# Position logits read from a turned copy of the queries, all between the key products

## The chip, the core and the metric

The kernel runs on one core of a Trainium2 chip. The metric is device time in microseconds (us), the median of several runs. A profiled execution gives a trace of every instruction, from which the views below are taken.

## What is computed

The input is eight images of 32 x 32 pixels with 512 channels. Two layers follow, each a group norm, an attention over all 1024 pixels and a residual sum. The first has 16 heads of 32 channels, the second 4 heads of 128 channels. Everything is in 32-bit floats. Only the second layer matters for the change. Cut to that:

```python
q = x @ Wq * scale
k = (x @ Wk).reshape(B, L, heads, kd).transpose(0, 2, 3, 1)
v = (x @ Wv).reshape(B, L, heads, kd).transpose(0, 2, 1, 3)
scores = attn_q @ k
pos = relative_logits(pos_q, pos_emb_w, pos_emb_h)
scores = scores + pos.reshape(B, heads, L, L)
attn = jax.nn.softmax(scores, axis=-1)
out = attn @ v
```

`relative_logits` adds, for a query at row x and column y of the image, one logit for each key column (from `pos_emb_w`, shifted by y) and one for each key row (from `pos_emb_h`, shifted by x). So all queries of one image column share a 32-wide window of `pos_emb_w`, and all queries of one image row share a window of `pos_emb_h`.

## The kernel before

Activations lie channels on partitions, pixels along the free dimension: a block is 128 partitions x 4 chunks x 1024 pixels. Blocks come from one pool with eight buffers (`block`, line 75). PSUM has a pool of three banks that most products share (`bank`, line 81), a tile `ps` of four banks with one buffer for the logits of the first layer (line 692), and one bank `acc`.

The 512 x 512 products with the weights are cut into halves and done with seven half-size products instead of eight (`seven`, line 407). A unit is one half of the output channels; its seven products go to three PSUM banks x, y and z in the order x, y, x, y, z, y, z. Each product is 16 TensorE passes (or 32 of half the length for the values), spread over four strips of 32 columns of the array (`by_columns`, line 327); a float matmul takes two passes. ScalarE, VectorE and GpSimd take the results out (lines 416 to 444 and the class `Plain`, lines 560 to 583): line 573 is ScalarE's copy of x, line 576 VectorE's sum from y, line 579 VectorE's sum from z, line 583 GpSimd's sum of two intermediate tiles, one of which is line 435's copy of z. All four quarters of a unit's output are there only when all four have run.

The first layer's attention (`attention_0`, line 685) runs in 64 steps a batch, and each step computes the logits of four heads into `ps` (line 698), takes their exponential on ScalarE (line 713), multiplies the exponentials of the step before with the values (line 724) and sums them on VectorE (line 736). Since `ps` has one buffer, line 698 of a step waits until line 713 of the step before has read it.

Between these steps `side_by_side` (line 1138) weaves the other work in by cost: each part yields how much it costs, and pieces are taken until their share of the total is reached. The other work of an iteration is, for the batch before, the rest of the first layer, the second layer's products (`second`, line 1058) and then the first batch's steps of the second attention (`attention_1`, line 811); the last batch runs its second layer with nothing beside it. `woven` (line 1126) lays a side sequence between the pieces of a main one: from piece `start` on, in each period of `gap` pieces, one piece of the side at each place in `places`.

`second` makes the queries, then the keys and the values with the position logits woven between. The position logits (`position_logits`, line 768) come in four groups a batch. A group takes one of the three shared banks, fills it with 16 matmuls (8 of line 782 for the image's columns, 8 of line 789 for its rows, 32 passes together, two strips for each line), casts four pieces of it to the block `posT` on ScalarE (line 802) and puts the four rests beside them on VectorE (line 807). The bank is free when the last of these has read it. With a start of 2 and a gap of 7, two groups stand between the keys' 14 products, two between the values'. Later line 822 adds the position logits to the second layer's logits.

Instructions are recorded in this order, and a scheduler then lays each engine's own sequence out and sets the waits; each engine runs its sequence in that order.

Of the kernel before, what the change touches and what calls it, by code (L numbers as in the profile page):

```python
# [27 lines left out]
def quick_path(  # L28
# [23 lines left out]
    nc = tc.nc  # L52

    B, IH, IW, C = x.shape
# [20 lines left out]
    def block(name, shape=None, dtype=F32):  # L75
        return mem.tile(shape or [P, CC, N], dtype, tag="block", name=name, bufs=BLOCKS)

    def chunks(block):
        return [block[:, i, :] for i in range(CC)]

    def bank(name, shape=None):
        return psum.tile(shape or [P, NB], F32, tag="bank", name=name, bufs=3)
# [38 lines left out]
    HC, HN = CC // 2, NB // 2  # L121
# [49 lines left out]
    ORDER = [0, 5, 1, 4, 6, 2, 3]  # L171
# [202 lines left out]
    def forms(x, name, room=None):  # L374
        got = []

        def whole():
            got.append((yield from forming(x, name, room)))

        run(whole())  # L380
        return got[0]
# [25 lines left out]
    def seven(fs, u, rows, sink, name, hook=None):  # L407

        product = taken(fs, u, rows)
        x = bank(f"x_{name}")
        product(x, 0, True)
        p1 = snapshot("e1", f"p1_{name}")
        nc.scalar.copy(p1, x)
        yield HC
        y = bank(f"y_{name}")
        product(y, 5, True)
        a = snapshot("es1", f"a_{name}")  # L420
        reader[0] = begun[0] = nc.vector.tensor_add(a, y, p1)
        sink.early(p1, a)
        yield HC
        product(x, 1, False)
        sink.c11(x)
        yield HC
        product(y, 4, False)
        b = snapshot("es1", f"b_{name}")
        reader[0] = half_done[0] = nc.vector.tensor_add(b, y, p1)
        sink.middle(b)  # L430
        yield HC
        z = bank(f"z_{name}")
        product(z, 6, True)
        p7 = snapshot("e1", f"p7_{name}")
        nc.scalar.copy(p7, z)  # L435
        yield HC
        product(y, 2, False)
        sink.c12(y, p1)
        if hook is not None:
            hook()  # L440
        yield HC
        product(z, 3, False)
        sink.c21(z, a)
        sink.c22(b, p7)
        yield HC
# [178 lines left out]
    def halves(x, u):  # L624

        return [[x[n * HC + u][:, h * NB : (h + 1) * NB] for h in range(NH)] for n in range(2)]

    def project_T(fs, m, y, name, units=(0, 1)):

        for u in units:  # L630
            stream.unit(m, False, u)
            yield from seven(fs, u, False, Plain(halves(y, u)), f"{name}_{u}")

    def project_rows(fs, m, y, name, hook=None, units=(0, 1)):

        for u in units:
            dst = [
                [y[:, h * (NT // 2) + 2 * u :, n * HN : (n + 1) * HN][:, :2] for h in range(NH)]
                for n in range(2)
            ]  # L640
            stream.unit(m, True, u)
            yield from seven(
                fs,
                u,
                True,
                Plain(dst, lambda t: t.rearrange("p (t n) -> p t n", n=HN)),
                f"{name}_{u}",
                hook if u else None,
            )
# [115 lines left out]
        yield 1  # L765
        finish(*state.pop("ended"))

    def position_logits(q, posT, b):

        qv = q.rearrange("p h (x y) -> p h x y", y=IW)
        by_y = posT.rearrange("p h (x s r) -> p r s h x", r=2, s=IW // 2)
        by_x = posT.rearrange("p h (s r y) -> p r s h y", r=2, s=IH // 2)
        G = NB // (IW * H1)
        for t in range(IW // (2 * G)):
            pp = bank(f"pp_{b}_{t}", [P, G, H1, 32])
            for g in range(G):
                for r in range(2):  # L780
                    s = 2 * (t * G + g) + r
                    nc.tensor.matmul(
                        pp[64 * r : 64 * r + 32, g],
                        pw_sb[:, IW - 1 - s : 2 * IW - 1 - s],
                        qv[:, :, :, s],
                        start=True,
                        stop=True,
                    )
                    nc.tensor.matmul(  # L789
                        pp[64 * r + 32 : 64 * r + 64, g],  # L790
                        ph_sb[:, IH - 1 - s : 2 * IH - 1 - s],
                        qv[:, :, s, :],
                        start=True,
                        stop=True,
                    )
            parts = []
            for r in range(2):
                for u, view in enumerate((by_y, by_x)):
                    view = view[:, r, t * G : (t + 1) * G]
                    rows = slice(64 * r + 32 * u, 64 * r + 32 * u + 32)  # L800
                    rests = slice(64 * (1 - r) + 32 * u, 64 * (1 - r) + 32 * u + 32)
                    nc.scalar.copy(view[rows], pp[rows])  # L802
                    parts.append((view[rests], pp[rows], view[rows].bitcast(F32)))

            yield -2
            for i, (rest, logits, greater) in enumerate(parts):
                nc.vector.tensor_sub(rest, logits, greater)  # L807
                if i % 2:
                    yield 0
# [248 lines left out]
    def second(b, st):  # L1058

        if "xn1" in st:  # L1060
            fs, sums = st.pop("xn1"), st.pop("sums1")
        else:
            fs, sums = forms(st.pop("x1"), f"xn1_{b}"), iter(())
        q = st["ao"] = block(f"q1_{b}")
        yield from woven(project_T(fs, WQ1, chunks(q), f"q1_{b}"), sums, 0, 2 * len(ORDER), (0, 3))
        posT = block(f"posT_{b}", dtype=F32R)
        k = chunks(block(f"k1_{b}"))
        v = block(f"v1_{b}", [P, NT, C])
        keys_and_values = chain(
            project_T(fs, WK1, k, f"k1_{b}"), project_rows(fs, WV1, v, f"v1_{b}")  # L1070
        )

        yield from woven(
            keys_and_values, position_logits(q, posT, b), 2, len(ORDER), (0, 1, 2)
        )
        st["at"] = (q, k, v, posT, b)

# [48 lines left out]
    def woven(main, side, start, gap, places=(0,)):  # L1126

        for at, cost in enumerate(main):
            if at >= start and (at - start) % gap in places:
                cost += next(side, 0)  # L1130
            yield cost
        yield from side
# [21 lines left out]
    def chain(*parts):  # L1154
        for part in parts:
            yield from part
# [20 lines left out]
    WP, WQ1, WK1 = Matrix(w_proj, 0, "p"), Matrix(Wq, 0, "q1"), Matrix(Wk, 0, "k1")  # L1177
# [45 lines left out]
    for b in range(B + 1):  # L1223
        rest, total = [], 0
        s = [None] * 2 + states + [None] * 2
# [9 lines left out]
        if last is not None:  # L1235
# [17 lines left out]
            else:  # L1253
                rest.append(chain(woven(other_keys(b, here), norm, 1, 1), marked()))
                total += PRODUCT // 2
            rest.append(later(second, b - 1, last))
            total += SECOND
            shared = here is not None and coming is None
# [522 lines left out]
```

## Time and profile before

| | |
|---|---|
| runs, us | 3816.88, 3814.26, 3814.05 (median 3814.26) |
| profiled execution, span from first to last instruction, us | 3815.0 |
| granted TensorE clock, mean | 0.998 |
| busy TensorE, VectorE, ScalarE, GpSimd, us | 3786.7, 2574.9, 1761.8, 660.0 |
| line 782, position logits of the columns | 512 passes, 69.7 us of union |
| line 789, position logits of the rows | 512 passes, 42.5 us of union |
| line 802, casts on ScalarE | 128, 106.1 us |
| line 807, subtractions on VectorE | 128, 112.0 us |

The profiled execution's own time is its span. The views call TensorE's matmuls PE, its weight loads PEld, VectorE DVE, ScalarE ACT, GpSimd POOL and SyncE SP. A row of a group has the line, engine and operation, output and inputs, shapes and count, then busy time in us and the mean in ns, then the engine's idle time just before and who ended it. A row of the timeline has the start in us from the span's start, the time it took, the instruction, and in brackets the idle time before it. Passes of TensorE overlap, and their ends are modelled, so its cost is read from the steps between starts.

### The profile page before, as it was taken

What the parts mean: (1) busy time and instruction counts of PE and PEld (TensorE: products, weight loads), DVE (VectorE), ACT (ScalarE), POOL (GpSimd) and SP (SyncE); (2) the same over time, 40 slices, a digit from 0 to 9 for tenths busy, and PEclk for the clock granted to TensorE, in tenths of its full rate; (3) what the DMA queues carried; (4) which work ended last, traced back from release to release, by engine and by line L of the source; (5) the groups of instructions that cost most, each with busy time, mean ns of one, the idle gap of its engine ahead of it and who ended that gap; (6) DMA issues with size and microseconds to landing.
All of it is one profiled execution on the core that took longest, in us unless ns stands there. A gap on an engine that the chain in (4) does not pass through costs nothing. (4 is left out here: it accounts for less than half of the span.)

```text
span 3815.0 us, 79937 instructions
## 1 busy us (share of the span) xinstructions
PE 3786.7 (99%) x34478; PEld 1376.4 (36%) x34478; DVE 2574.9 (67%) x2967; ACT 1761.8 (46%) x1830; POOL 660.0 (17%) x397
## 2 busy tenths in 40 slices
PE   9999999999999999999999999999999999999998
PEld 4232244323443234432343323433234332334353
DVE  6778665586656866569665686656866569665545
ACT  2555544445444454444544445444454445553132
POOL 1342101131101310013111131111310113001201
PEclk9999999999999999999999999999999999999999
DMA  6132120232202312034120241103411033110321
GB/s 186 62 105 70 39 56 10 71 102 53 56 12 92 86 46 56 16 93 93 38 53 19 94 95 40 45 23 98 91 41 40 26 98 77 33 37 31 110 41 26
DMA packets 482985, 234.74 MB, mean 62 GB/s; under 512 B 269600, under 2 KB 461376, under 8 KB 481600
## 3 DMA queue, kind: packets, MB, share of 16 engines
q1 hardware_dynamic: 470992, 213.74, 20.8%
q0 software_dynamic: 2608, 13.70, 1.0%
q8 instruction: 274, 4.49, 0.5%
q10 hardware_dynamic: 9024, 2.10, 0.3%
q14 instruction: 87, 0.71, 0.1%
HBM read 170.72 MB, written 58.72 MB: 60 GB/s over the span
## 5 line engine op out<-in xcount | busy, mean ns | idle before, releaser
L736 DVE TENSOR_TENSOR e_room<-e_room 128x2048 f32<-128x2048 f32 x448 | 1078.6, 2407 | 396.4 <-ACT e_room L713 393.7
L713 ACT ACTIVATE e_room<-ps 128x2048 f32<-128x2048 f32 x512 | 961.8, 1879 | 788.5 <-PE ps L698 744.2
L698 PE MATMUL ps<-q,k 32*64 32x512 f32 x8192 | 577.7, 613 | 0.2 <-ACT e_room L713 0.2
L724 PE MATMUL acc<-e_room,v 128*32 128x512 f32 x4096 | 545.8, 604 | 0.0
L824 ACT ACTIVATE e<-ps 128x512 f32<-128x512 f32 x512 | 305.7, 597 | 507.4 <-PE ps L822 436.3
L821 PE MATMUL ps<-q,k 128*128 128x512 f32 x1024 | 525.0, 594 | 0.2 <-DVE posT L807 0.2
L833 PE MATMUL acc<-e,v 128*128 128x512 f32 x1024 | 522.0, 593 | 0.3 <-ACT e L824 0.3
L679 POOL TENSOR_TENSOR q<-q,su 128x512 f32<-128x512 f32 x127 | 198.2, 1560 | 1524.8 <-DVE su L675 1423.5
L844 DVE TENSOR_TENSOR es<-es,e 128x512 f32<-128x512 f32 x384 | 290.5, 757 | 250.9 <-ACT e L824 248.3
L822 PE MATMUL ps<-posT,sel 128*128 128x512 f32 x512 | 406.6, 794 | 0.0
L821 PEld LDWEIGHTS ps<-q,k 128*128 128x128 f32 x1024 | 192.6, 190 | 230.1 <-issue 218.5
L698 PEld LDWEIGHTS ps<-q,k 32*64 32x64 f32 x8192 | 120.4, 129 | 391.3 <-issue 223.1
L833 PEld LDWEIGHTS acc<-e,v 128*128 128x128 f32 x1024 | 193.1, 189 | 147.3 <-issue 92.6
L724 PEld LDWEIGHTS acc<-e_room,v 128*32 128x32 f32 x4096 | 81.3, 108 | 411.4 <-issue 364.1
L659 DVE STREAM_TRANSPOSE tu<-su 128x512 f32<-128x512 f32 x128 | 90.6, 708 | 98.2 <-ACT su L657 96.5
L822 PEld LDWEIGHTS ps<-posT,sel 128*128 128x128 f32 x512 | 97.3, 190 | 122.5 <-issue 122.5
L657 ACT COPY su<-sums 128x512 f32<-128x512 f32 x128 | 74.9, 585 | 131.1 <-PE sums L746 81.3
L807 DVE TENSOR_TENSOR posT<-pp,posT 32x512 fp32r<-32x512 f32 x128 | 112.0, 875 | 32.2 <-ACT posT L802 30.9
L583 POOL TENSOR_TENSOR k<-b_k,p_k 128x512 f32<-128x512 f32 x32 | 50.7, 1584 | 477.7 <-ACT p_k L435 467.0
L802 ACT CAST posT<-pp 32x512 fp32r<-32x512 f32 x128 | 106.1, 829 | 46.0 <-PE pp L789 44.9
L583 POOL TENSOR_TENSOR v<-b_v,p_v 128x512 f32<-128x512 f32 x32 | 51.5, 1611 | 436.5 <-ACT p_v L435 436.5
L583 POOL TENSOR_TENSOR q<-b_q,p_q 128x512 f32<-128x512 f32 x32 | 67.9, 2121 | 255.2 <-ACT p_q L435 255.2
(223 smaller groups left out, 4542.3 us busy)
## 6 DMA issues: line engine op xcount, KB each, us to landing
w_qkv<-ws_qkv SPq DMA_DIRECT2D x168, 128.0 KB, 2.5
d<-x0T SPq DMA_DIRECT2D x32, 512.0 KB, 3.2
x1T<-d SPq DMA_DIRECT2D x32, 512.0 KB, 5.7
d<-x1T SPq DMA_DIRECT2D x32, 512.0 KB, 3.6
x2T<-d SPq DMA_DIRECT2D x32, 512.0 KB, 6.2
w_qkv<-in_L_conv_w_qkv SPq DMA_DIRECT2D x126, 128.0 KB, 2.2
out<-ot SPq DMA_DIRECT2D x240, 64.0 KB, 2.0
xs<-in_x SPq DMA_DIRECT2D x224, 64.0 KB, 2.5
```

The source lines that it names most:

```text
L583: nc.gpsimd.tensor_tensor(self.dst[1][1], s(b), s(p7), op=ALU.add)
L679: engine.tensor_tensor(dst, dst, su, op=ALU.mult)
L698: nc.tensor.matmul(ps[some, r, :], k[m][rows, j * P + 64 * i : j * P + 64 * i + 64], q[m][rows, h * NB : (h + 1) * NB], start=True, stop=True,
L713: nc.scalar.activation(e, ps, AF.Exp, scale=D0 ** -0.5)
L724: nc.tensor.matmul(acc[r * D0 : (r + 1) * D0, :], v[:, j, c0 : c0 + D0], e[:, r, :], start=(j == blocks[0]), stop=(j == blocks[-1]),)
L736: summed[0] = nc.vector.tensor_add(state["esum"], state["esum"], e)
L807: nc.vector.tensor_sub(rest, logits, greater)
L821: nc.tensor.matmul(ps, k[h][:, keys], q[:, h, queries], start=True, stop=False)
L822: nc.tensor.matmul(ps, sel_flat[:, keys], posT[:, h, queries], start=False, stop=True)
L824: nc.scalar.activation(e, ps, AF.Exp, scale=1.0 / math.sqrt(D1))
L833: nc.tensor.matmul(acc, v[:, j, h * D1 : (h + 1) * D1], e, start=(j == 0), stop=(j == NT - 1),)
L844: added[0] = nc.vector.tensor_add(state["esum"], state["esum"], e)
```

## The change

A new block `turned` gets a copy of the second layer's queries in which each image is turned over: pixels column by column instead of row by row. ScalarE makes it, one chunk of 128 x 1024 at a time, two after each of the queries' two units, four a batch. Line 782 (783 in the changed kernel) reads its queries from there: for one image column, 32 elements in a row for each of four heads, where it read 128 elements that were 32 apart. The matmuls, their number, shapes and results are the same. The gap of the weave becomes 3, so that all four groups of position logits stand between the keys' products, from the third on, one group every three products, and none between the values'.

```diff
-    def position_logits(q, posT, b):
+    def position_logits(q, turned, posT, b):
...
         qv = q.rearrange("p h (x y) -> p h x y", y=IW)
+        tv = turned.rearrange("p h (y x) -> p h y x", x=IH)
...
                         pw_sb[:, IW - 1 - s : 2 * IW - 1 - s],
-                        qv[:, :, :, s],
+                        tv[:, :, s, :],
...
         q = st["ao"] = block(f"q1_{b}")
-        yield from woven(project_T(fs, WQ1, chunks(q), f"q1_{b}"), sums, 0, 2 * len(ORDER), (0, 3))
+        turned = block(f"turned_{b}")
+
+        def queries():
+            for u in range(2):
+                yield from project_T(fs, WQ1, chunks(q), f"q1_{b}", (u,))
+                for m in (u, u + HC):
+                    nc.scalar.copy(
+                        turned[:, m, :].rearrange("p (y x) -> p y x", x=IH),
+                        q[:, m, :].rearrange("p (x y) -> p y x", y=IW),
+                    )
+
+        yield from woven(queries(), sums, 0, 2 * len(ORDER), (0, 3))
...
         yield from woven(
-            keys_and_values, position_logits(q, posT, b), 2, len(ORDER), (0, 1, 2)
+            keys_and_values, position_logits(q, turned, posT, b), 2, 3, (0, 1, 2)
         )
```

## The prediction

> **What bounds the kernel now.** I read the page's busy shares first, then the groups by line, then the timeline of one batch of the second layer.
>
> ```profile
> PE 3786.7 (99%) x34478; PEld 1376.4 (36%) x34478; DVE 2574.9 (67%) x2967; ACT 1761.8 (46%) x1830; POOL 660.0 (17%) x397
> L713 ACT ACTIVATE e_room<-ps 128x2048 f32<-128x2048 f32 x512 | 961.8, 1879 | 788.5 <-PE ps L698 744.2
> L698 PE MATMUL ps<-q,k 32*64 32x512 f32 x8192 | 577.7, 613 | 0.2 <-ACT e_room L713 0.2
> ```
>
> PE is busy for 99% and its idle time before the first layer's logits (L698) is 0.2 us. So a PE microsecond removed is one gained, and a PE wait added is one lost. ACT idles, but its exponentials (L713, 1.88 us) work on one PSUM tile `ps` (one buffer), so the next L698 waits for the exponential before. The timeline of batch 2's queries, second unit, shows the room:
>
> ```profile
> 1360.58 0.59 ACT L435 COPY p_q<-z_q 128x512 f32<-128x512 f32 x1 [0.85 <-PE z_q L331]
> 1361.25 2.70 POOL L583 TENSOR_TENSOR q<-b_q,p_q 128x512 f32<-128x512 f32 x1 [0.58 <-ACT p_q L435]
> ...
> 1362.74 0.68 DVE L576 TENSOR_TENSOR q<-y_q,p_q 128x512 f32<-128x512 f32 x1
> ...
> 1363.33 1.88 ACT L713 ACTIVATE e_room<-ps 128x2048 f32<-128x2048 f32 x1 [2.16 <-PE ps L698]
> ...
> 1365.24 2.29 DVE L736 TENSOR_TENSOR e_room<-e_room 128x2048 f32<-128x2048 f32 x1 [1.82 <-ACT e_room L713]
> 1365.87 1.11 PE L698 MATMUL ps<-q,k 32*64 32x512 f32 x16
> ...
> 1367.45 0.68 DVE L579 TENSOR_TENSOR q<-z_q,a_q 128x512 f32<-128x512 f32 x1
> ```
>
> The exponential ends at 1365.21 and the next L698 starts at 1365.87: 0.66 us to spare.
>
> The operation that the change is about:
>
> ```profile
> L782 PE MATMUL pp<-q,pw_sb x512: 393/433/452, 431.1 to 3639.6; 128*32 128x128 f32 x171
> ```
> ```profile
> L789 PE MATMUL pp<-q,ph_sb x512: 272/273/299, 431.1 to 3639.0; 128*32 128x128 f32 x171
> ```
> (ns, least/median/most.) L782 moves 128 queries 32 elements apart, L789 the same number in runs of 32: 433 against 273 ns. ACT pays for such steps too. Of the four casts of one group, the first writes 32 elements apart, the second runs:
>
> ```profile
> L802 ACT CAST posT<-pp x1: 1087/1087/1087, 1377.2 to 1377.2; 32x512 fp32r<-32x512 f32 x1
> ```
> ```profile
> L802 ACT CAST posT<-pp x1: 576/576/576, 1378.3 to 1378.3; 32x512 fp32r<-32x512 f32 x1
> ```
>
> [...]L583 took 2.70 us beside L736 above, 1.28 us at its quickest. [...]the trace's ACT copies of 512 and exponentials of 2048 elements (585, 1879 ns) give 0.842.
>
> **PE's gain.** A group of position logits is 32 passes (16 matmuls, two passes each) in four column strips side by side, eight to a strip. A strip of L782 starts its passes on average 0.249 us apart (first to last start 1.68 to 1.79 us for seven steps), so a group takes 1.99 us; where the column strips of L789 are not held back, theirs start 0.109 us apart (1374.99, 1375.10, 1375.21, 1375.32). With both in runs: 8 x 0.109 = 0.87 us. There are 8 batches x 4 groups: 32 x (1.99 - 0.87) = **35.8 us gained**. Bounds: nothing below 0.87 is shown. From above, products with 256 columns run 32 passes in 1.73 us, so PE can be fed at least this fast: a gain of at least 32 x 0.26 = 8 us. I take 35.8, since L789's strips did run at 0.109 with all four strips in flight.
>
> **The copies on ACT.** 32 are added (two a unit, two units a batch), 128 x 1024, read 32 apart and written in a row. The trace shows no such read. Lower end: in a row, 585 + 512 x 0.842 = 1.02 us[...]. Upper end: the cast's surcharge, (1087 - 576)/512 = 1.0 ns an element, 1.02 + 1.02 = 2.04. I take 2.0, because L782 shows the surcharge on reads and the cast shows it on ACT. 32 x 2.0 = 64 us of ACT time, which its idle 54% could hold; what costs is the place. In the built order of the changed kernel the first copy stands ahead of the exponential that follows the unit's sixth product, and waits for POOL L583 and DVE L576; the second waits for DVE L579. All exponentials queue behind.
>
> Walk through the unit above. POOL ends at 1363.95; the copy runs 1364.0 to 1366.0; the exponential ends at 1367.9 instead of 1365.21; the next L698 starts at 1368.0, not 1365.87: **2.1 us lost** (copy + 0.1). The sum on DVE (L736) stands ahead of L579 and needs that exponential: it ends at 1370.2, L579 at 1370.9, the second copy at 1372.9, the next exponential at 1374.8. PE meanwhile has attention (0.88) and two products (1.83 + 1.72) and would go on at 1373.5: **1.45 lost** (copy - 0.57). So 3.55 a unit: the second unit of batches 1 to 5, 17.8 us. Batch 0's first unit has one product there instead of two: 2.1 + 3.15 = 5.2; its second has two and a sum, 2.1 + 0.4 = 2.5. In the first unit of batches 1 to 5 both copies stand ahead of one exponential: in batch 2, L576 ends at 1343.34, copies to 1347.4, exponential to 1349.3, next L698 at 1349.35 instead of 1346.54: 2.8 x 5 = 14. Batch 6, with other attention steps between, 3.1 + 2; batch 7 has no exponentials: 0.4. Sum: 17.8 + 7.7 + 14 + 5.1 + 0.4 = **45 us lost**. With 1.02 us copies the same walk gives 18.
>
> **The closer groups.** They now come every three products instead of seven. A group holds one of three PSUM banks until its four casts (3.36 us) and four subtractions (3.53, begun after the last cast) are done: 7 us. The built order of batch 2, from the start of the product ahead of group one: PE does that product (to 1.7), the group (2.6), two products (6.1), L698 and attention (8.0), a product (9.8), and wants a bank for group two. ACT casts group one from 2.8 to 6.1, DVE subtracts from 6.15 to 9.7: free in time. Group two ends at 10.7; a product, attention and two products follow (17.9), while its casts end at 14.2 and its subtractions at 17.8: in time again. Behind group three's casts (19.0 to 22.3) and a copy stands an exponential that could start at 21.8 and starts at 22.9; the next L698 wants its end at 24.3 and gets it at 24.9, 0.6 us late. Group four, wanted at 28.6, finds its bank free since 25.9. So 0.7 x 7 = 5 us. In batch 7, without attention between, group two is wanted three products after group one, at 7.75, and gets the bank at 9.7; group three is wanted at 15.8 and gets it at 17.8; before group four a product waits 0.9 for a copy behind the casts, and the group 1.9 for the subtractions: 6.8 us. Before the change, a bank made PE wait some 0.4 us there four times:
>
> ```profile
> 3618.10 1.93 PE L331 MATMUL x_v<-w_v,x1T 128*32 128x256 f32 x32 [0.25 <-PE z_k L331]
> ```
>
> That is 6.8 - 1.7 = 5. Together **10 lost** (bounds 3 and 31: nothing late but batch 7 in part; or 1 us more for each of 21 groups). The value products, free of groups, no longer wait for a bank: in six batches the last ran 0.4 us long, **2.4 back**. The moved steps issue no DMA, and L802 and L807 are the same instructions as before. The tile `turned` takes one of eight blocks; the values' block needs it back, and the last group has read it before the first value product, so no wait. Weight loads on SP keep their order, and its queue is passed by nothing.
>
> **Sum** on the profiled execution: 3815.0 - 35.8 + 45 + 10 - 2.4 = 3831.8. Its span is 0.7 above the median (3814.26) with nothing that matters around it, so 3831.
>
> **Rivals.**
> - *The copies are cheap*: 1.02 us each, 18 lost instead of 45: 3804. For it: no read 32 apart by ACT is in the trace. Against: PE reads and ACT writes both pay. The sign turns at about 1.4 us a copy. This is the one that ends faster.
> - *PE is fed too slowly*: with L782's reads mended, 32 weight loads and 32 passes take 1.73 us a group, gain 8: 3859. For it: L698 takes 1.044 us for 16 passes[...]. Against: the 0.109 us steps.
> - *The banks bind*: the 0.1 us margins are lost, 1 us at 21 groups: 3852. For it: margins so thin; DVE's L736 can take 3.05 us instead of 2.29. Against: that was beside POOL, which is not due there.
>
> **Chances.** Forecast 0.56 (own range 3822 to 3843), cheap copies 0.22, slow feed 0.10, banks 0.12. The measurement tells 0.2%, 7.6 us: under 3806.6 is faster, over 3821.9 slower. Faster: most of the cheap copies and a little of the forecast, 0.17; same: their rest and the forecast's low end, 0.13; slower 0.70. The range goes from the cheap copies' 3803 to 3855 between the last two; outside it are half of those cases' chances at most.
>
> **What would show it.** L783's matmuls at 273 ns and groups near 0.9 us; the copies (line 1072) at 2.0 us; "L698 <- ACT e_room" with waits of 2 to 3 us some 26 times, in the queries' stretch alone; small waits in the keys' stretch. Wrong if the copies take 1.0 us, if L698 doesn't wait for ACT though they take 2, or if a group stays near 2 us.

## The result and the profile after

| kernel | median, us | range | executions |
|---|---|---|---|
| before | 3814.16 | 3813.34 to 3816.88 | 4 |
| changed | 3839.46 | 3835.74 to 3840.41 | 4 |

The changed kernel is slower by 25.3 us: ratio 1.0063, 95% interval 1.0049 to 1.0077. The forecast was 3831 (3803 to 3855).

The page of the changed kernel, whose lines answer to the first three that were shown of before (line numbers behind the new line 774 are one higher):

```profile
span 3833.9 us, 80001 instructions
...
PE 3760.0 (98%) x34478; PEld 1350.4 (35%) x34478; DVE 2577.0 (67%) x2967; ACT 1820.0 (47%) x1862; POOL 667.2 (17%) x397
...
L713 ACT ACTIVATE e_room<-ps 128x2048 f32<-128x2048 f32 x512 | 961.9, 1879 | 719.6 <-PE ps L698 684.7
...
L698 PE MATMUL ps<-q,k 32*64 32x512 f32 x8192 | 578.7, 613 | 33.8 <-ACT e_room L713 33.8
```

PE works 26.7 us less, yet the span is 18.9 us longer: its idle time went from 28.3 to 73.9 us. The last line says where most of that lies: ahead of L698 it was idle for 33.8 us, ended by ACT's exponential L713. Before it was 0.2.

The rows of the operation that was mended, with least, median and most in ns:

```profile
L783 PE MATMUL pp<-turned,pw_sb x512: 269/273/297, 436.7 to 3638.6; 128*32 128x128 f32 x171
```
```profile
L790 PE MATMUL pp<-q,ph_sb x512: 272/273/298, 436.7 to 3638.6; 128*32 128x128 f32 x171
```

L783 now costs what L790 costs, 273 ns. The passes of a strip start 0.109 us apart (0.764 us, the median, for seven steps), and in 31 of the 32 groups the product behind a group begins 0.87 to 0.90 us after the group's first pass (the other one is taken up below).

The copies, and below them ACT's idle time ahead of them with what ended it (us, times):

```profile
L1072 ACT COPY turned<-q x32: 1932/1984/2052, 394.7 to 3608.6; 128x1024 f32<-128x1024 f32 x32
...
  DVE q L576: 25.1, 9
  DVE q L579: 21.0, 7
  POOL q L583: 19.2, 7
```

A copy takes 1.98 us, and ACT stood still for 25.1 + 21.0 + 19.2 = 65 us with one at the head of its queue. The timeline of the stretch that was shown of before, batch 2's queries, second unit (start, time, instruction, idle time before it):

```profile
1368.86 2.76 POOL L583 TENSOR_TENSOR q<-b_q,p_q 128x512 f32<-128x512 f32 x1 [0.52 <-ACT p_q L435]
...
1371.65 2.03 ACT L1072 COPY turned<-q 128x1024 f32<-128x1024 f32 x1 [2.87 <-POOL q L583]
...
1373.59 1.87 ACT L713 ACTIVATE e_room<-ps 128x2048 f32<-128x2048 f32 x1
1375.48 2.29 DVE L736 TENSOR_TENSOR e_room<-e_room 128x2048 f32<-128x2048 f32 x1 [4.40 <-ACT e_room L713]
...
1375.50 1.12 PE L698 MATMUL ps<-q,k 32*64 32x512 f32 x16 [1.90 <-ACT e_room L713]
...
1377.69 0.68 DVE L579 TENSOR_TENSOR q<-z_q,a_q 128x512 f32<-128x512 f32 x1
1378.20 2.83 PE L331 MATMUL x_k<-x1T,w_k 128*32 128x512 f32 x16
...
1378.46 1.98 ACT L1072 COPY turned<-q 128x1024 f32<-128x1024 f32 x1 [3.01 <-DVE q L579]
...
1380.34 1.87 ACT L713 ACTIVATE e_room<-ps 128x2048 f32<-128x2048 f32 x1
```

Read it as a chain: the sum on POOL ends at 1371.62 and the copy starts; the exponential, whose logits were there at 1370.89, follows it (ACT's 1862 instructions start in this trace in the order in which the program has them, without exception); the next L698 waits 1.90 us for that exponential. DVE's sum L736 needed it too, so L579 and the second copy are late in turn. One row doesn't fit: the product at 1378.20 took 2.83 us, where such a product takes 1.90. That is taken up below.

### The profile page after: what moved, and what is told of

Read it like the earlier page. It is cut to its first block, busy times and chain, and to the rows that moved or that the text cites. A ratio compares the mean times of both kernels' runs of the same rounds, so it can differ in the third digit from the quotient of the medians.

```text
span 3833.9 us, 80001 instructions
## 1 busy us (share of the span) xinstructions
PE 3760.0 (98%) x34478; PEld 1350.4 (35%) x34478; DVE 2577.0 (67%) x2967; ACT 1820.0 (47%) x1862; POOL 667.2 (17%) x397
## 5 line engine op out<-in xcount | busy, mean ns | idle before, releaser
L736 DVE TENSOR_TENSOR e_room<-e_room 128x2048 f32<-128x2048 f32 x448 | 1079.8, 2410 | 450.1 <-ACT e_room L713 446.6
L713 ACT ACTIVATE e_room<-ps 128x2048 f32<-128x2048 f32 x512 | 961.9, 1879 | 719.6 <-PE ps L698 684.7
L698 PE MATMUL ps<-q,k 32*64 32x512 f32 x8192 | 578.7, 613 | 33.8 <-ACT e_room L713 33.8
L698 PEld LDWEIGHTS ps<-q,k 32*64 32x64 f32 x8192 | 120.6, 130 | 423.3 <-issue 227.2
L583 POOL TENSOR_TENSOR k<-b_k,p_k 128x512 f32<-128x512 f32 x32 | 51.7, 1615 | 489.1 <-ACT p_k L435 439.8
L808 DVE TENSOR_TENSOR posT<-pp,posT 32x512 fp32r<-32x512 f32 x128 | 111.5, 871 | 35.3 <-ACT posT L803 33.7
L583 POOL TENSOR_TENSOR v<-b_v,p_v 128x512 f32<-128x512 f32 x32 | 55.2, 1726 | 375.3 <-ACT p_v L435 369.5
L583 POOL TENSOR_TENSOR q<-b_q,p_q 128x512 f32<-128x512 f32 x32 | 68.2, 2130 | 264.3 <-ACT p_q L435 254.8
```

Of the source, the lines that this page charges most:

```text
L583: nc.gpsimd.tensor_tensor(self.dst[1][1], s(b), s(p7), op=ALU.add)
L698: nc.tensor.matmul(ps[some, r, :], k[m][rows, j * P + 64 * i : j * P + 64 * i + 64], q[m][rows, h * NB : (h + 1) * NB], start=True, stop=True,
L713: nc.scalar.activation(e, ps, AF.Exp, scale=D0 ** -0.5)
L736: summed[0] = nc.vector.tensor_add(state["esum"], state["esum"], e)
```

## Where the time went, by parts

The start and the end of an execution vary by themselves: the first L698 starts at 62.15 us in the profile of before, where TensorE's clock was at half speed for 10.2 us ahead of it, and at 60.02 in that of the changed kernel, where it was not. So the parts are compared over the stretch from the start of the first L698 to that of the last product, 3741.0 us before and 3763.4 after (+22.3). Parts of the change were run alone (e1 to e9, below), and the same stretch is read from their traces. The medians are each taken against the kernel before that ran beside it:

| part | from | predicted | measured in the stretch | by medians |
|---|---|---|---|---|
| reads in runs | e3 less before | -35.8 | -35.4 | -34.3 |
| closer groups, with what is given back | e8 less e3 | +10 - 2.4 | +11.5 | +10.4 |
| copies on ACT | changed less e8 | +45 | +46.2 | +49.2 |
| sum | | +16.8 | +22.3 | +25.3 |

The medians of the third part come from different sessions. The two executions of the changed kernel that ran beside e8 (e7, below) lie 54.2 above e8's median.

## The experiments

Diffs are against the changed kernel, unless said otherwise. Times are medians; that of the kernel before, run beside them, was 3814.7 to 3814.8.

### e1: the gap alone

Diff against the kernel before:

```diff
-            keys_and_values, position_logits(q, posT, b), 2, len(ORDER), (0, 1, 2)
+            keys_and_values, position_logits(q, posT, b), 2, 3, (0, 1, 2)
```

> The kernel before with the gap of the weave at 3, and nothing else: no copies, line 782 reads 32 apart as before. Theory (copies cost 45 us, closer groups 10, reads gain 36): 3814 + 10 - 2.4, about 3822 (3817 to 3828), since the groups still take 2 us each. Rival (the closer groups, with their three banks, carry the loss of some 60 us, and the copies are hidden in ACT's idle half): 3860 or more.

Measured: 3825.41 us (3824.48 to 3826.80), ratio 1.0028 [1.0017, 1.0038], +10.7. The groups' nearness costs some 10 us and the banks don't bind at every group: the rival fell.

### e2: the copies alone

```diff
-        tv = turned.rearrange("p h (y x) -> p h y x", x=IH)
...
-                        tv[:, :, s, :],
+                        qv[:, :, :, s],
...
-            keys_and_values, position_logits(q, turned, posT, b), 2, 3, (0, 1, 2)
+            keys_and_values, position_logits(q, turned, posT, b), 2, len(ORDER), (0, 1, 2)
```

> The kernel before with the four copies a batch on ACT where the changed kernel has them, read by nobody; gap 7, reads 32 apart. Theory: 3814 + 45, about 3859 (3850 to 3866), the waits of PE for the exponential in the queries' stretch alone. Rival (closer groups carry the loss): 3814 to 3822.

Measured: 3866.03 us (3861.76 to 3869.54), ratio 1.0133 [1.0117, 1.0150], +51.3. Its page:

```profile
L698 PE MATMUL ps<-q,k 32*64 32x512 f32 x8192 | 579.5, 614 | 35.6 <-ACT e_room L713 35.6
```

With nobody reading the copies, PE waits as in the changed kernel. So the loss comes from the place of the copies in ACT's queue and not from their result being late. It is 6 us more than the walk of the prediction gave, with a spread of 7.8 us where before has 3.4; what e7 shows accounts for most of it.

### e3: the reads alone

```diff
-        tv = turned.rearrange("p h (y x) -> p h y x", x=IH)
+        tv = q.rearrange("p h (y x) -> p h y x", x=IH)
```

No copies, and the gap is `len(ORDER)` again.

> The kernel before, but line 782 reads runs of 32 queries from the queries themselves, as if they had been turned over; the turning over is left out, so the logits of the columns belong to other pixels. Gap 7, no copies. Theory: 32 groups shorter by 1.1 us each: 3814 - 36 = 3778 (3774 to 3782). Rival (PE is fed no faster than a pass in 54 ns): 3806.

Measured: 3780.39 us (3778.56 to 3781.73), ratio 0.9907 [0.9890, 0.9923], -34.3. The gain of PE is whole, to 4% of the forecast. That PE is fed too slowly (a gain of 8) fell.

### e4: copies in a row

```diff
-                        turned[:, m, :].rearrange("p (y x) -> p y x", x=IH),
-                        q[:, m, :].rearrange("p (x y) -> p y x", y=IW),
+                        turned[:, m, :],
+                        q[:, m, :],
```

> The changed kernel with copies that do not turn the image over (read and written in a row), in the same place and with the same waits; the logits of the columns then belong to other pixels. Theory: a copy takes 1.02 us instead of 1.98 and the walk's loss falls from 45 to 18 us: 3839 - 27 = 3812 (3806 to 3818). Rival (the loss is the waiting for POOL and DVE ahead of the exponential, whatever the copy's length): 3833 to 3839.

Measured: 3808.01 us (3806.16 to 3810.56), ratio 0.9982 [0.9975, 0.9989]. The copy's row and, from the page, the waits:

```profile
L1072 ACT COPY turned<-q x32: 1040/1045/1057, 397.1 to 3583.4; 128x1024 f32<-128x1024 f32 x32
```
```profile
L698 PE MATMUL ps<-q,k 32*64 32x512 f32 x8192 | 578.4, 613 | 15.1 <-ACT e_room L713 15.1
```

The same instructions at the same places, 0.94 us shorter each, cost 17 us over e8 instead of 49. This is the rival of cheap copies carried out; its price was 3804. It was the copy's duration that decided the sign.

### e5 and e6: the copies on other engines

```diff
-                    nc.scalar.copy(
+                    nc.gpsimd.tensor_copy(
```

and in e6 `nc.vector.tensor_copy(`.

> The changed kernel with the 32 turning copies on GpSimd instead of ScalarE, in the same places. Theory (the loss is that the exponentials queue behind the copies): the 45 us go, the gain of the reads and the 10 us of the closer groups stay: 3814 - 34 + 11 = 3791 (3786 to 3800, the top if GpSimd's copies hold up DVE's sums). Rival (the copies cost through the time at which `turned` is there, or through their traffic): 3820 or more.

> The changed kernel with the turning copies on VectorE. Theory: some 1.9 us a copy by line 807's rate; the exponentials no longer queue behind them, but DVE's sums and the sums of the products do, and DVE is busy for 67%: 3791 plus up to one us a copy, 3791 to 3815. Rival (any engine's copies cost the same): 3835.

Measured: e5 3789.97 us (3789.45 to 3790.61), ratio 0.9936 [0.9919, 0.9952]; e6 3790.91 us (3789.84 to 3791.69), ratio 0.9939 [0.9922, 0.9955]. The copies' rows, e5 and then e6:

```profile
L1072 POOL COPY turned<-q x32: 1942/1984/2047, 394.8 to 3561.8; 128x1024 f32<-128x1024 f32 x32
```
```profile
L1072 DVE COPY turned<-q x32: 1059/1093/1132, 394.9 to 3562.0; 128x1024 f32<-128x1024 f32 x32
```

From e5's page:

```profile
L698 PE MATMUL ps<-q,k 32*64 32x512 f32 x8192 | 577.7, 613 | 1.9 <-ACT e_room L713 1.9
```

A POOL copy takes the same 1.98 us as ACT's, and PE waits for L713 for 1.9 us in all, as in e8 without any copy (2.0): what stands behind it in POOL's queue is not on PE's path. So the 49 us are the price of ACT's queue, not of the copies' work. In e6 the copies stand among the sums of DVE, and there too is room for them, at 1.09 us each where 1.9 had been expected.

### e8: reads and gap, no copies

As e3, with the gap of 3.

> The changed kernel without its copies: line 782 reads runs of 32 from the queries themselves (the turning over is left out, so the logits of the columns belong to other pixels), gap 3. Theory: the closer groups cost 10 us with short groups as with long ones: 3780 + 10 = 3790 (3786 to 3794). If short groups come too close for three banks, more: 3800.

Measured: 3790.81 us (3790.79 to 3791.15), ratio 0.9938 [0.9921, 0.9955]. Over e3 the closer groups cost 10.4, as in e1 (10.7), so the parts add up; e5 is within 1 us of it, so copies on POOL are free.

### e7: the changed kernel again

No edit.

> The changed kernel once more, for a second profile. Its profiled execution spanned 3833.9 while the median of its runs is 3839.5. [...]POOL's sum (line 583) and the waits behind the copies are longer here in an execution of 3839 than in the first profile; if not, the 5 us lie outside the waits.

Measured: 3845.04 us (two executions, 3844.12 and 3845.95), ratio 1.0080 [1.0060, 1.0100]. That POOL's sums and the waits are longer here fell: the sums of the queries (L583) take 2.13 us on average in both profiles, the copies 1.987 us against 1.984, and PE's waits are as in the first. What differs is TensorE's clock. The trace's clock records show it at half speed for a time. In the kernel before this happens only at the start and the end of an execution. In the changed kernel it also happens behind PE's waits, for 3.41 us at a time. The busy times in four stretches of the first profile (from and to, their length, then busy us of PE, PEld, DVE, ACT and POOL, PE's granted clock, DMA share and GB/s):

```profile
1349.35:1352.77 3.42, 2.34 (x24) 0.52 (x16) 0.00 (x0) 3.42 (x3) 0.00 (x0) 1.00 0.46 83
1352.77:1356.18 3.41, 1.98 (x28) 0.57 (x32) 2.00 (x1) 2.55 (x3) 0.00 (x0) 1.00 0.25 58
1373.25:1376.66 3.41, 1.51 (x24) 0.34 (x24) 1.18 (x1) 2.20 (x2) 0.00 (x0) 1.00 0.12 38
1376.66:1380.07 3.41, 3.41 (x20) 0.85 (x23) 1.71 (x2) 1.61 (x1) 0.00 (x0) 0.50 0.02 5
```

and of two in e7's:

```profile
1359.51:1362.92 3.41, 1.05 (x12) 0.13 (x4) 0.00 (x0) 3.41 (x3) 0.00 (x0) 1.00 0.40 81
1362.92:1366.33 3.41, 3.28 (x24) 0.73 (x28) 2.29 (x1) 1.66 (x3) 0.00 (x0) 0.50 0.00 0
```

Within a profile all the starts of half clock lie whole multiples of 3.41333 us apart, to 0.01 us (in the first at 1376.66, 1847.70, 2318.74, 2789.78, 3250.58 and, at the end, 3827.43). So I cut the traces of the changed kernel, e7, e1, e2 and e4 on that grid and took PE's idle time in each slice, by the modelled ends of its passes. After 18 slices with 1.83 to 2.90 us of it, the next slice ran at half clock; after none with less than 1.83; from 1.83 to 1.94 both occur. (Once half clock went on for a second slice.) In e3, e5, e6, e8 and both of e9, no slice between the start and the end had more than 1.93 us, and none ran at half clock. The rows show it in batch 2: in the first profile the first unit's wait of 2.52 us fell across two slices (idle 3.42 - 2.34 = 1.08, and 1.43), and the clock stayed. In e7 the same wait lay in one slice (idle 3.41 - 1.05 = 2.36), and the clock fell to 0.50. In the second unit it was the other way round: idle 1.90 and then 0.50 in the first profile, idle 1.83 and full clock in e7. Which waits were hit depended, in these two profiles, on where the grid lay.

What such a slice of half clock, a hit, costs: PE's work in it takes 1.4 to 1.7 us longer. In the first profile four of the five hits stood where PE would have waited 1.29 us for the second copy's exponential anyway, and cost 0.3 each; the fifth, in batch 6, 1.4. That is some 2.5 us of the stretch's +46.2. In e7 most hits stand behind first units, where no other wait hides them, and the stretch is 7.8 us longer than in the first profile. The mean clock of the changed kernel's six executions goes with their times: 0.997 (3835.7 and 3838.5), 0.996 (3840.4 twice), 0.995 (3844.1 and 3845.9). But this mean takes in the start and the end too, where half clock lasts longer in one execution than in another (at the start 0 us in the first profile, 6.8 in e7's). That the grid is the cause comes from the traces of these runs; no run shifted it on purpose. e4 points the same way: most of its waits behind copies last 0.64 or 0.92 us, none of its waits behind copies draws half clock, and its 18 executions lie within 4.4 us. Its one hit follows a wait of 1.96 us that the closer groups make (batch 0, below).

### e9: groups a little farther apart

e5 with a gap of 4, and with a gap of 5:

```diff
-            keys_and_values, position_logits(q, turned, posT, b), 2, 3, (0, 1, 2)
+            keys_and_values, position_logits(q, turned, posT, b), 2, 4, (0, 1, 2)
```

> The kernel with the copies on GpSimd, groups every four products instead of three (the fourth behind the first value product). Theory: in batch 7 a group is wanted 4 x 1.72 us after the one before, near the 7 us that its bank is held, so the four waits of 1.8 us there shrink below 0.5, and the 0.4 us waits behind the third group go: 3790 - 8 = 3782 (3779 to 3786). Rival (the 10 us come from elsewhere than the banks and casts): 3790.

> The same with groups every five products, the last in the value products. Theory: no wait for a bank is left: 3780 (3778 to 3783), as with the reads alone. Against: the values' block takes the place of the turned one, and a value product's copy waits for the last group: then above 3783.

Measured: gap 4 3783.23 us (3782.43 to 3784.04), ratio 0.9915 [0.9898, 0.9932]; gap 5 3786.40 us (3785.82 to 3787.33), ratio 0.9924 [0.9908, 0.9941]. Gap 4 is the fastest kernel here that turns the queries over, 0.85% under before. The waits for a bank in batch 7 fall from 5.3 us in e5 to 0.2, as the theory had it, but waits of products behind products there grow from 1.4 to 4.0, which it had not; most of the gain is 0.9 us in each of batches 1 to 5. Gap 5 missed its forecast by 6 us. Its timeline of PE in batch 2, behind the fourth group:

```profile
1411.82 1.07 PE L698 MATMUL ps<-q,k 32*64 32x512 f32 x2
1412.82 1.93 PE L331 MATMUL z_v<-w_v,x1T 128*32 128x256 f32 x32
1414.57 1.91 PE L331 MATMUL y_v<-w_v,f_xn 128*32 128x256 f32 x32
1416.41 1.11 PE L698 MATMUL ps<-q,k 32*64 32x512 f32 x14
```

The scheduler put one of the eight logits matmuls of a step (two passes) ahead of two products. Alone it holds PE for 1.00 us, and the other seven (14 passes) still take as long as all eight, 1.04. Behind the fourth group that happens seven times, in batches 0 to 6, and not at all with gap 4: 7.0 us. Without it gap 5 would stand at 3786.4 - 7.0 = 3779.4, near its forecast of 3780; that was not run. The case against, a wait for the block of the turned queries, had forecast a time above 3783 too, but PE is idle for 29.0 us in all, as in e3 (29.1), so such a wait isn't what was lost.

## Why the prediction was right

**PE's gain: right.** 35.8 forecast, 35.4 in the stretch and 34.3 by medians. The strips of both lines keep the 0.109 us a step that the forecast took from L789, with all four strips in flight. Its 0.249 us for L782 spanned the line's two strips; within one strip the steps are 0.247 us, which makes the gain 35.3. For its rival of a slow feed: the rounds of 512-column passes of L331 start 0.429 us apart in the trace of before, so two of them take 0.858 us where the 16 passes of L698 take 1.044.

**The copies' price: right.** 2.0 forecast, 1.98 measured; a read 32 elements apart costs ACT about what the cast's write did (1.98 us against 1.045 in a row in e4, 0.9 ns an element more, against 1.0). That ACT pays on reads too was an estimate of the forecast, from L782's reads and L802's writes. It was the largest doubt, and e4 shows that the sign hung on it. For DVE the runs settle less. Its copies took 1.09 us in e6, but none was run there in a row. Its subtractions do pay: in the changed kernel a piece of L808 that is 32 elements apart took 1.05 us, the next, in runs, 0.69:

```profile
L808 DVE TENSOR_TENSOR posT<-pp,posT x1: 1051/1051/1051, 3617.3 to 3617.3; 32x512 fp32r<-32x512 f32 x1
```
```profile
L808 DVE TENSOR_TENSOR posT<-pp,posT x1: 686/686/686, 3618.4 to 3618.4; 32x512 fp32r<-32x512 f32 x1
```

One reading of before was loose: the L736 that ran beside L583 is not the row shown at 1365.24 but the one before it (1359.77, 3.05 us). In that trace the 282 L736 with nothing on POOL beside them take at most 2.29 us, the 166 with something there up to 3.37; L583 takes 1.28 us with nothing on DVE beside it (twice), with something there up to 3.32.

**The waits behind the copies: right in place and size.** What PE lost by place, in the changed kernel's trace (the wait that the timeline shows, and some 0.06 us by which passes would else have overlapped):

| place | predicted | measured |
|---|---|---|
| batch 0, first unit | 5.2 | 1.88 + 2.96 = 4.84 |
| batch 0, second unit | 2.5 | 1.19 + 1.72 = 2.91 |
| batches 1 to 5, first unit, each | 2.8 | 2.58 |
| batches 1 to 5, second unit, each | 2.1 + 1.45 = 3.55 | 1.96 + 1.29 = 3.25 (batch 1) |
| batch 6 | 5.1 | 7.35 |
| batch 7 | 0.4 | 0.2 |

Batches 2 to 5 lost 1.9 + 1.57 in the second unit, at half clock. The sum is 45.5 of 45, and that it is so close is in part luck: 2.5 of it is half clock, for which the forecast had nothing, and the waits themselves are shorter than forecast. Batch 6 is the one place that was well over: in its second unit PE's row sums L746 waited 2.77 us for ACT's L739, which stood behind a copy and an exponential, and a hit of half clock added 1.4. The count in the last paragraph of the forecast was wrong: there are 17 waits of 1.1 to 2.9 us (15 of L698, two of L746), not 26 of 2 to 3; its own walk has about 21.

**The closer groups: right mechanism, too small.** 7.6 net forecast, 11.5 measured. Batch 7, where nothing stands between the groups, shows the bank at work (PE's, ACT's and DVE's rows of the timeline):

```profile
3614.02 3.28 ACT L803 CAST posT<-pp 32x512 fp32r<-32x512 f32 x4 [0.29 <-PE pp L790]
...
3617.20 1.90 PE L331 MATMUL y_k<-f_xn,w_k 128*32 128x512 f32 x16
3617.33 3.48 DVE L808 TENSOR_TENSOR posT<-pp,posT 32x512 fp32r<-32x512 f32 x4 [0.90 <-ACT posT L803]
...
3620.95 0.27 PE L783 MATMUL pp<-turned,pw_sb 128*32 128x128 f32 x1 [1.85 <-DVE posT L808]
```

The casts start at 3614.02, the subtractions end at 3620.81: the bank is held for 6.8 us, where the forecast had 7, and the next group waits 1.85 for it (2.0 forecast). The sum of e8 over e3: 6.8 ahead of the groups, some 6 of it in batch 7, as forecast there; 2.6 + 2.0 ahead of L698 and of the product after attention in the keys' stretches, two small waits of 0.4 where the forecast saw one of 0.7. 1.6 more lie behind the groups, for which it had nothing: in batch 0 a product waits 1.97 us for DVE's sum L429, which stands in DVE's queue behind the subtractions of a group and an L736. Another 1.2 lie between products, in batch 7 and in batch 6, where it had nothing. Back came 2.4 from the value products, as forecast. The thin margins of 0.1 us held: no 1 us at every group, so the rival of binding banks fell in e1 and e8.

**The term that was missing: half clock.** The sum had PE's waits at their length and nothing for the clock that falls behind them. On the grid of 3.413 us that e7 shows, some 1.9 us of idle time in a slice was enough for a slice at 0.50. Half clock makes up some 2.5 us of the first profile's stretch. The forecast also took before's span (3815.0) as its base, while that execution itself took 3816.88, the longest of its runs; as a span is some 1.9 us shorter than its execution, the two nearly cancel, and the forecast amounts to 16.8 over the median.

In sum: the medians moved by 25.3 us and not by 16.8. Of the 8.5 between them 3.9 are the closer groups and 2.5 the half clock in the profiled execution. Another 3.0 is what the medians lie further apart than the stretch; that it is half clock too, behind waits or at the start, is argued from the lower mean clocks of the other executions, not shown. The waits behind the copies, 1.3 shorter than forecast, and the gain, 0.4 smaller, make up the rest.

## What to carry to other kernels

Cost a copy by what stands behind it in its engine's queue, not by the engine's idle share: 32 copies of 2 us cost some 50 us on an ACT that was idle for half its time and nothing on POOL. If a copy must share a queue with what feeds TensorE, its duration less the slack there is what each one costs (0.94 us less for each of 32 brought the loss from 49 us to 17, e4), so measure a strided read first. When a change lets TensorE wait 2 us at a time, add up to 1.7 us for each such wait, because here its clock could fall to half behind it.

## What had not been expected of the hardware

- Half clock for 3.41 us on a grid of 3.413 us, behind slices in which PE was idle for 1.83 to 2.90 us (18 hits).
- DVE copies 128 x 1024 floats that are read 32 apart in 1.09 us (e6), close to ACT's copy in a row (1.045 us, e4), while ACT and POOL both take 1.98 us for it.
- One of eight matmuls that run side by side in the array takes 1.00 us alone, all eight 1.04, and the seven that are left 1.04: splitting such a set costs its whole time (e9, gap 5).
